# A graph network on one Trainium2 core: which copies and additions of edge counts wait for each other in the first layer's loop

## The chip, the core and the metric

The kernel runs on one core of a Trainium2 chip. The metric is the time of one execution on the device in microseconds; the time given for a kernel is the median of several runs. A profiled execution is a run of its own and takes longer than the others, so durations from it are compared with its own time.

## What is computed

3125 nodes carry rows of 256 numbers, and 100,000 edges (src, dst) join them. The edges arrive sorted by dst, with far more edges at low numbers of dst. Four layers follow each other, each added to its input: a graph attention network of two attention layers, a mixture of experts with one routing for all nodes, two graph convolutions, and a mixture of experts that routes each node. The change lies in the first attention layer and in what it shares with the later ones:

```python
h = (x @ W).reshape(N, H, C)                       # H = 4 heads
e = leaky_relu(al_s[src] + al_d[dst], 0.2)
alpha = exp(e - m[dst]) / segment_sum(exp(e - m[dst]), dst)
out = segment_sum(h[src] * alpha[:, :, None], dst) + bias
```

The later attention layer and the convolutions need only how often each pair (src, dst) occurs. The first layer's loop makes that table of counts while it also forms the first layer's sums.

## The kernel before

`FirstLayer.run` (L2093) holds the loop. Three kinds of work are woven together in it, step by step.

*Counting.* The edges are cut into 391 chunks of 256. Since dst is sorted, the edges of one chunk fall into a narrow window of dst: 8, 14 or 20 columns wide, by the chunk's number (`width`, L80). `make` (L1663) writes two one-hot tiles for a chunk: hot_key (which block of 128 src nodes, and which column of the window) on VectorE (DVE, L1669), and hot_lo (which node within the block) on DVE (L1672) for every third chunk and the first 20, and otherwise on ScalarE (ACT, L1675 and L1678). `multiply` (L1681) multiplies the two on TensorE (PE) into one of three PSUM banks, ps; the product holds the chunk's counts, 128 partitions by 25 blocks by the window's columns. Two instructions bring it into the running table acc, in float16. `keep` (L1697) copies all columns of the window but the first to their place on ACT (L1703); nothing was there before, because the edges are sorted. `add` (L1705) adds the first column on DVE (L1708), because the chunk before may have counted in that column too. The window's place is read from a table into a register when the kernel runs, so the code that sets the waits doesn't know which columns are touched: it sees two instructions that both write somewhere in acc.

`count_step(i)` (L1738) puts them in this order: make chunk i, multiply chunk i-1, add chunk i-3, copy chunk i-2. So each addition waits for the copy just before it, which is that of its own chunk, and each copy waits for the addition just before it, which is that of the chunk before. A bank of ps is free for another product once its addition has read it.

The table is made in ten pieces of 320 dst columns. At the first chunk of a piece `keep` calls `piece` (L1650), which clears a new acc tile on DVE (L1659) and copies over the 100 columns that the old one holds beyond its end (L1661). The finished piece has the nodes' own edges added (`add_own`, L1710) and is stored (`store_counts`, L1719).

*Edges.* For the 283 chunks from number 108 on, `edge_step` (L1883) sums the first layer directly. GpSimd (POOL) fetches the rows of the edges' src (L1797), SyncE (SP) loads windows of terms (L1807, L1810). Four chunks make a batch. For a batch DVE forms the places (L1820, L1823), PE picks the terms (L1831), DVE adds them (L1840, L1843), ACT takes their exponential edge_p (L1844), and DVE spreads it (L1849). For each chunk PE multiplies (L1863, L1869) and DVE adds the sums (L1880). Finished pieces go through the first weights (`through_w1`, L1956), whose results ACT copies out (L1999).

*Dense part.* Once the first piece of counts is stored, 100 steps (`dense_step`, L2077) handle the first 256 dst nodes: exponentials on ACT (L2029, L2031), a product with the counts on DVE (L2036), and a multiplication on PE (L2045).

In the loop each pass calls `count_step`, one waiting task, and as many edge and dense steps as are due, until all are through; counting ends first. The instructions of PE, DVE and ACT are chained in exactly the order in which they are written (`in_order`, L108), so an engine never goes around an instruction that waits. In front of the loop the same `count_step` is called 20-odd times among the layer's preparations; there only DVE's order is fixed by hand. Among those preparations are the exponential of own_w on ACT (L1614), its store to loops, and its loads from there.

Of the kernel before, what the change touches and what calls it, by code (L numbers as in the profile page):

```python
# [17 lines left out]
ALU = mybir.AluOpType  # L18
AX = mybir.AxisListType
PSUM = bass.MemoryType.PSUM  # L20
SYNC = mybir.DependencyInfo(mybir.DependencyClass.Sync, mybir.DependencyReason.DATA)
# [58 lines left out]
def width(c):  # L80
    return next(w for a, e, w in WIN if a <= c < e)
# [7 lines left out]
class Kernel:  # L89
    def __init__(self, ctx, tc):  # L90
        self.tc, self.nc = tc, tc.nc
        nc = self.nc
        self.const = const = ctx.enter_context(tc.tile_pool(name="const", bufs=1))
        self.dram = ctx.enter_context(tc.tile_pool(name="dram", bufs=1, space=DRAM))
        self.ident = const.tile([P, P], F32, name="ident")
        make_identity(nc, self.ident)
        self.eps = const.tile([P, 1], F32, name="eps")
        nc.vector.memset(self.eps, EPS)


        self.rows = const.tile([P, NB, D + 1], F32, name="x_rows")
        self.x = self.rows[:, :, :D]

        self.counts = self.dram.tile([NB, P, NP], F32, name="counts")

        self.counts_t = self.dram.tile([NB, P, NB, P], F32, name="counts_t")
# [1287 lines left out]
class FirstLayer:  # L1394
# [10 lines left out]
    def __init__(self, k, I):  # L1405
        self.k, self.nc, self.tc, self.I = k, k.nc, k.tc, I
        self.table = k.dram.tile([NP, D + 8], F32, name="table")
        self.terms = k.dram.tile([1, NP * 4], F32, name="terms")

        self.places = k.dram.tile([NC, CE], F32, name="places")  # L1410

        self.turned = k.dram.tile([P, 2, NP], F32, name="x_turned")
        self.loops = k.dram.tile([NP - DN, 4], F32, name="loops")
        self.inverse = k.dram.tile([AS, 4, GA], F32, name="inverse")
        self.first = k.dram.tile([4, P, 2, NP], F32, name="first_out")
        self.deg_row = k.dram.tile([NB, P], F32, name="deg_row")
        self.tasks, self.regs, self.counted = deque(), {}, False

# [273 lines left out]
        return g, o  # L1694


    def keep(self, c):  # L1697
        g, o = self.place_of(c)
        if c == CUT[g] and g:
            self.piece(g)  # L1700
            self.tasks.appendleft(lambda: self.store_counts(g - 1))
            self.tasks.appendleft(lambda: self.add_own(g - 1))
        self.nc.scalar.copy(self.acc[g][:, :, ds(o + 1, width(c) - 1)], self.parts[c][:, :, 1:])  # L1703

    def add(self, c):  # L1705
        g, o = self.place_of(c)
        col = self.acc[g][:, :, ds(o, 1)]
        self.nc.vector.tensor_tensor(col, col, self.parts.pop(c)[:, :, 0:1], ALU.add)  # L1708

    def add_own(self, g):  # L1710

# [379 lines left out]


    def run(self, src_cols, dst_cols, dst_rows, x_in, keep, stats, u2):  # L2093

        tc, nc, k, I = self.tc, self.nc, self.k, self.I
# [606 lines left out]
```

## Time and profile before

| what | value |
| --- | --- |
| median of 3 runs | 2530.82 us (2530.34 to 2532.02) |
| the profiled execution's own time | 2636.26 us |
| its span, first to last instruction | 2634.5 us |
| mean granted TensorE clock in it | 0.931 |
| PE busy over the span | 2263.8 us (86%) |
| DVE busy | 1376.1 us (52%) |
| ACT busy | 1153.5 us (44%) |
| POOL busy | 833.4 us (32%) |
| first and last copy of counts (L1703) | 68.9 and 1076.7 us |
| 391 copies L1703 | 178.1 us busy, 455 ns each |
| 391 additions L1708 | 256 ns each (median) |
| 782 one-hots hot_key L1669 | 324 ns each between 60 and 1077 us |
| 494 first halves of hot_lo on ACT, L1675 | 391 ns each |
| 247 second halves, L1678 | 416 ns each |
| 782 products L1686 | 356 ns each |

How to read it: an engine is busy while it executes an instruction; the time before an instruction in which its engine stood idle is given with what ended it, found from the semaphores. A line such as "ACT acc L1703 <- DVE acc L1708: 111.9, 80, 17.6" says that ACT, before its instruction of line 1703 that writes acc, stood idle for 111.9 us in total, in 80 cases, at most 17.6 us, until DVE's instruction of line 1708 ended. In a timeline a line gives start and length in us, engine, line, operation, what it writes and reads, and in brackets the idle time ahead of it. PEld is TensorE's loading of weights; a q behind an engine's name means its sequencer, which handles register operations and separate waits while the engine itself is idle or at work on something earlier.

### The profile page before, as it was taken

Reading aid. Unit: us, or ns where it says so; the run is one execution under the profiler, and the core shown is the slowest. Engines: PE = TensorE matmul, PEld = TensorE weight load, DVE = VectorE, ACT = ScalarE, POOL = GpSimd, SP = SyncE. Lnnn points to the kernel's source line nnn. Section 1 sums busy time; section 2 is a strip of 40 time slices with the busy share of each in tenths; the row PEclk is TensorE's granted clock in tenths of the full one; section 3 lists DMA queues with packets and bytes.
Section 4 is the critical chain, followed back from the end, with each engine's and each line's share of the span. In section 5 each row is a group of like instructions: output and inputs, shape, how many; then the busy total and the mean of one; then the engine's idle time right before and its main releaser. Section 6 shows DMA issues by size and latency. Waiting matters only on the chain. (4 is left out here: it accounts for less than half of the span.)

```text
span 2634.5 us, 38636 instructions
## 1 busy us (share of the span) xinstructions
PE 2263.8 (86%) x11821; PEld 1827.0 (69%) x11821; DVE 1376.1 (52%) x4332; ACT 1153.5 (44%) x2553; POOL 833.4 (32%) x805
## 2 busy tenths in 40 slices
PE   4277789888888888598999989979999998999997
PEld 4155566666666665387888768868877666888886
DVE  6666657466776786514888833433335654111110
ACT  3167655545555554342444434543433434222221
POOL 1465566666676775010000030000001122212221
PEclk9977988888989998899999989989999988999998
DMA  6633446464656665499221110004324426666662
GB/s 219 88 103 89 128 108 183 114 179 119 173 158 175 190 175 149 131 378 304 81 75 63 50 36 0 1 31 145 114 100 139 140 100 195 168 186 180 175 193 54
DMA packets 241723, 354.97 MB, mean 135 GB/s; under 512 B 45360, under 2 KB 182931, under 8 KB 237794
## 3 DMA queue, kind: packets, MB, share of 16 engines
q1 hardware_dynamic: 197762, 253.10, 30.6%
q0 software_dynamic: 40176, 94.81, 14.2%
q10 hardware_dynamic: 3568, 4.47, 0.7%
q8 instruction: 99, 1.62, 0.3%
q14 instruction: 118, 0.97, 0.1%
HBM read 266.60 MB, written 86.86 MB: 134 GB/s over the span
## 5 line engine op out<-in xcount | busy, mean ns | idle before, releaser
L1797 POOL DMA_INDIRECT edge_rows<-table,pick x566 | 608.7, 1075 | 320.2 <-PE edge_sums L1863 107.6
L1863 PE MATMUL edge_sums<-edge_moves,edge_rows 128*128 128x120 f32 x2264 | 351.6, 305 | 37.1 <-DVE agg L1880 30.6
L1863 PEld LDWEIGHTS edge_sums<-edge_moves,edge_rows 128*128 128x128 f32 x2264 | 327.2, 217 | 74.3 <-DVE agg L1880 41.6
L1092 PE MATMUL po<-parts,cnt_r 128*128 128x512 f32 x1250 | 328.2, 416 | 9.4 <-ACT cnt_r L1086 9.4
L1686 PE MATMUL ps<-hot_key,hot_lo 128*128 128x350 f16 (+2 forms) x782 | 205.3, 356 | 106.1 <-DVE acc L1708 49.2
L1703 ACT CAST acc<-ps 128x325 f32 (+2 forms) x391 | 178.1, 455 | 255.5 <-DVE acc L1708 111.9
L1092 PEld LDWEIGHTS po<-parts,cnt_r 128*128 128x128 f32 x1250 | 239.4, 197 | 70.6 <-ACT cnt_r L1086 10.2
L854 PE MATMUL po<-h,w 128*128 128x257 f32 x1250 | 277.5, 382 | 6.7 <-DVE w L845 4.4
L854 PEld LDWEIGHTS po<-h,w 128*128 128x128 f32 x1250 | 236.5, 191 | 43.1 <-DVE w L845 6.4
L1669 DVE TENSOR_SCALAR hot_key<-iota_key,key 128x350 f16<-128x350 f16 (+2 forms) x782 | 231.5, 324 | 34.1 <-PE ps L1686 25.6
L2578 ACT ACTIVATE hid<-ph,ffn_b 128x256 f32<-128x256 f32 x232 | 109.9, 474 | 298.2 <-PE ph L2576 298.2
L2576 PE MATMUL ph<-xe,ffn_w 128*128 128x256 f32 x928 | 210.1, 382 | 2.0 <-DVE xe L2555 2.0
L2586 PE MATMUL py<-ffn_w,hid 128*128 128x256 f32 x928 | 209.5, 384 | 0.0
L2590 POOL DMA_INDIRECT out<-y,to x58 | 90.4, 1558 | 350.1 <-DVE y L2589 269.1
L2576 PEld LDWEIGHTS ph<-xe,ffn_w 128*128 128x128 f32 x928 | 173.9, 191 | 28.9 <-DVE xe L2555 2.2
L2586 PEld LDWEIGHTS py<-ffn_w,hid 128*128 128x128 f32 x928 | 176.5, 193 | 23.4
L1686 PEld LDWEIGHTS <-hot_lo 128*128 128x128 f16 x782 | 62.4, 104 | 160.0 <-issue 60.4
L839 ACT ACTIVATE z<-z,att_cols 128x640 f32<-128x640 f32 x125 | 103.1, 828 | 153.0 <-DVE z L837 130.1
L1675 ACT ACTIVATE hot_lo<-iota_key,lo 128x128 f16<-128x128 f16 x494 | 169.0, 391 | 0.0
L1880 DVE TENSOR_TENSOR agg<-agg,edge_sums 128x126 f32 (+1 forms) x283 | 87.0, 307 | 145.4 <-PE edge_sums L1869 43.9
L1086 ACT CAST cnt_r<-cnt_h 128x1920 fp32r<-128x1920 f16 x50 | 89.9, 1799 | 133.4 <-PE po L1092 130.4
L2045 PE MATMUL po<-x_rows,w 128*128 128x257 f32 x400 | 129.5, 451 | 3.6 <-issue 3.6
(403 smaller groups left out, 3368.2 us busy)
## 6 DMA issues: line engine op xcount, KB each, us to landing
ffn_w<-in_L_ffn_W SPq DMA_DIRECT2D x58, 1024.0 KB
cnt_h<-cnt SPq DMA_DIRECT2D x50, 800.0 KB
rows<-blank SPq DMA_DIRECT2D x109, 258.0 KB
cnt<-acc SPq DMA_DIRECT2D x50, 400.0 KB
cnt<-cnt SPq DMA_DIRECT2D x25, 800.0 KB
normed<-first_out SPq DMA_DIRECT2D x20, 640.0 KB
first_out<-first SPq DMA_DIRECT2D x56, 192.0 KB
edge_rows<-table,pick POOLq DMA_INDIRECT x566
```

The costliest lines, as they stand in the source:

```text
L854: nc.tensor.matmul(pos[i][:, :D + 1], lhsT=w[:, ts(i, P)], rhs=moving[:, j, :D + 1], start=(j == 0), stop=(j == NB - 1))
L1092: nc.tensor.matmul(pos[b], lhsT=c[:, j - j0, ts(b, P)], rhs=parts[i][:, j].rearrange("p a m -> p (a m)"), start=(j == 0), stop=(j == NB - 1))
L1669: nc.vector.tensor_scalar(h[:, u, :NB * w], self.wide[:, :NB * w], self.key[:, t:t + 1], None, op0=ALU.is_equal)
L1675: nc.scalar.activation(l[:, u, :], self.wide[:, :P], AF.Abs, bias=self.lo[:, t:t + 1], scale=-1.0)
L1686: self.nc.tensor.matmul(ps[:, :n], lhsT=l[:, u, :], rhs=h[:, u, :n], start=(u == 0), stop=(u == CT - 1))
L1703: self.nc.scalar.copy(self.acc[g][:, :, ds(o + 1, width(c) - 1)], self.parts[c][:, :, 1:])
L1797: self.nc.gpsimd.indirect_dma_start(out=self.ring[:, e % (RB * BT), :], out_offset=None, in_=self.table, in_offset=bass.IndirectOffsetOnAx ...
L1863: nc.tensor.matmul(ps[:, f * 4 * w:f * 4 * w + EW], lhsT=self.rows_of(m)[:, e, ts(f, P)], rhs=self.spread[m % 2][:, e * 4 * w:e * 4 * w + EW],
L2045: self.nc.tensor.matmul(self.pos[i][:, :D + 1], lhsT=w[:, ts(i, P)], rhs=self.k.rows[:, j, :], start=(j == 0), stop=(j == NB - 1))
L2576: nc.tensor.matmul(ph, lhsT=w1[:, c, ts(f, P)], rhs=xe[:, c, :], start=(c == 0), stop=(c == 1))
L2578: nc.scalar.activation(hid[:, f, :], ph, AF.Gelu, bias=b1[:, f:f + 1])
L2586: nc.tensor.matmul(py, lhsT=hid[:, f, ts(i, P)], rhs=w2[:, f, :], start=(f == 0), stop=(f == NF - 1))
```

## The change

Copies and additions are put into a group named "columns", whose members no longer wait for each other on account of acc. In place of that, each addition is told by name to wait for two copies: that of its own chunk and that of the chunk ahead of it (c-1). Copies are told to wait for no addition. The wait of a copy for its matmul, of both for `piece`, and of anything outside the group for them stays as it was. No instruction that computes is added or left out, and the order in which the functions are called is the same.

```diff
@@ -1414,7 +1414,7 @@
         self.inverse = k.dram.tile([AS, 4, GA], F32, name="inverse")
         self.first = k.dram.tile([4, P, 2, NP], F32, name="first_out")
         self.deg_row = k.dram.tile([NB, P], F32, name="deg_row")
-        self.tasks, self.regs, self.counted = deque(), {}, False
+        self.tasks, self.regs, self.kept, self.counted = deque(), {}, {}, False
 
 
 
@@ -1694,18 +1694,27 @@
         return g, o
 
 
+
+
     def keep(self, c):
         g, o = self.place_of(c)
         if c == CUT[g] and g:
             self.piece(g)
             self.tasks.appendleft(lambda: self.store_counts(g - 1))
             self.tasks.appendleft(lambda: self.add_own(g - 1))
-        self.nc.scalar.copy(self.acc[g][:, :, ds(o + 1, width(c) - 1)], self.parts[c][:, :, 1:])
+        self.kept[c] = self.nc.scalar.copy(self.acc[g][:, :, ds(o + 1, width(c) - 1)],
+                                           self.parts[c][:, :, 1:])
+        self.tc.declare_no_dep(self.kept[c].ins, group="columns",
+                               reason="no copy takes an earlier window's first column")
 
     def add(self, c):
         g, o = self.place_of(c)
         col = self.acc[g][:, :, ds(o, 1)]
-        self.nc.vector.tensor_tensor(col, col, self.parts.pop(c)[:, :, 0:1], ALU.add)
+        ins = self.nc.vector.tensor_tensor(col, col, self.parts.pop(c)[:, :, 0:1], ALU.add)
+        self.tc.add_to_no_dep_group("columns", ins.ins)
+        for b in (c - 1, c):
+            if b >= 0:
+                self.tc.add_manual_dep(ins.ins, self.kept[b].ins.name, SYNC)
 
     def add_own(self, g):
 
```

## The prediction

> **What bounds the kernel now.** I began with the busy time by stretch of the first layer's loop (the columns are the stretch, its length, then busy us and count of PE, PEld, DVE, ACT and POOL, the granted clock, the DMA share and GB/s):
>
> ```profile
> 136.00:215.00 79.00, 60.67 (x394) 48.22 (x394) 54.40 (x265) 54.67 (x177) 46.84 (x47) 0.76 0.37 97
> 215.00:300.00 85.00, 63.06 (x444) 46.22 (x442) 58.98 (x269) 58.34 (x181) 48.17 (x46) 0.84 0.41 113
> 300.00:500.00 200.00, 165.44 (x1105) 129.82 (x1103) 116.12 (x443) 107.31 (x291) 128.58 (x126) 0.88 0.49 134
> 900.00:1077.00 177.00, 146.42 (x945) 108.04 (x944) 130.84 (x399) 95.08 (x241) 103.77 (x103) 0.92 0.55 159
> ```
>
> No engine is full. From 136 to 300 us PE, DVE and ACT are each busy for 69 to 77% of the time and wait for each other in turn; from 300 us PE, at 83%, is nearest to a bound. Then the waits of ACT from 60 to 1077 us (us in total, times, longest):
>
> ```profile
> ACT acc L1703 <- DVE acc L1708: 111.9, 80, 17.6
> ACT edge_p L1844 <- DVE edge_p L1843: 74.8, 42, 6.2
> ACT acc L1703 <- DVE acc L1661: 20.9, 8, 4.7
> ```
>
> The first line is what the change removes; the other two stay. 111.9 us is not a gain: ACT has slack. So I asked who is late because ACT is. From 136 to 300 us PE's waits and DVE's read:
>
> ```profile
> PE ps L1686 <- ACT hot_lo L1678: 10.6, 17, 1.1
> PE ps L1686 <- DVE acc L1708: 8.9, 12, 2.1
> PE ps L1686 <- ACT hot_lo L1675: 2.7, 3, 1.1
> ```
> ```profile
> DVE acc L1708 <- ACT acc L1703: 11.3, 24, 2.6
> ```
>
> Last, I followed the chain of waits back from 1077 us, where counting ends, at each step to what released it. It runs through a copy (L1703) 63 times; 16 of these copies were released by an addition (L1708). Two cases from the timeline. One pays:
>
> ```profile
> 268.56 0.25 DVE L1708 TENSOR_TENSOR acc<-acc,ps 128x25 f32 x1
> 268.90 0.46 ACT L1703 CAST acc<-ps 128x325 f32 x1 [0.71 <-DVE acc L1708]
> 269.24 0.69 ACT L1675 ACTIVATE hot_lo<-iota_key,lo 128x128 f16<-128x128 f16 x2
> 269.96 0.42 ACT L1678 ACTIVATE hot_lo<-hot_lo 128x256 f16<-128x256 f16 x1
> 270.43 0.47 PE L1686 MATMUL ps<-hot_key,hot_lo 128*128 128x350 f16 x2 [1.11 <-ACT hot_lo L1675]
> ```
>
> The copy waits 0.71 us for an addition of the chunk before it, the one-hot behind it is late, and PE stands for 1.11 us. One doesn't:
>
> ```profile
> 970.34 0.24 DVE L1708 TENSOR_TENSOR acc<-acc,ps 128x25 f32 x1
> 970.68 0.55 ACT L1703 CAST acc<-ps 128x475 f32 x1 [3.30 <-DVE acc L1708]
> 970.90 0.19 DVE L1843 SCALAR_TENSOR_TENSOR edge_p<-edge_p,edge_rows 128x32 f32<-128x32 f32 x1
> 971.19 0.23 ACT L1844 ACTIVATE edge_p<-edge_p 128x32 f32<-128x32 f32 x1
> 971.33 0.68 ACT L1675 ACTIVATE hot_lo<-iota_key,lo 128x128 f16<-128x128 f16 x2
> ```
>
> Without its 3.30 us the copy ends earlier, but ACT's next instruction needs DVE's L1843, which ends at 971.09.
>
> [...] everything behind the copy at 970.68 stood with it. [...] DVE's sequencer dealt with the waits of L1840 from 604.94 to 605.29 us, while L1840 itself started at 605.75.
>
> **The change part by part.**
>
> *Copies lose the wait for DVE.* In the built program only copies at the starts of pieces still have one (behind L1661). Each of the 16 links can save at most the lesser of two times: how long ACT stood idle before the copy, and how long the copy's matmul had been done. From 136 to 300 us there are 11 links, 2.43 + 0.69 + 0.04 + 0.48 + 0.68 + 0.68 + 0.39 + 0.77 + 0.39 + 0.71 + 0.79 = 8.05 us. At the first, 139.7 us, PE stood only 0.87 us for ACT afterwards, so 0.87 replaces 2.43: 6.5 us. The upper end is PE's whole wait for ACT's one-hots there, 10.6 + 2.7 = 13.3 us, if ACT gets far enough ahead. I take 8 us, near the lower end: the 6.5 counts one chain alone, and ACT also gets ahead off it (22 such waits, 14.7 us, in this stretch), but a parallel chain may be close behind. From 300 us there are 5 links, 0.07 + 0.89 + 3.30 + 1.46 + 2.96 = 8.7 us. The three large ones are caught again: at 971 and 853 us by the exponential L1844, at 603 us by PE's need for L1823, which DVE, never idle there, ends at 604.60. I take 1 us; the ends are 0 and 8.7.
>
> *Additions.* They waited for their own copy before and still do; the copy of the chunk ahead (c-1) is earlier on ACT and costs nothing. But a wait that used to be implied, for DVE's own previous addition, is now explicit: 297 additions get a separate wait instruction on DVE, and ACT loses 202 of 307. Their prices are in the records by line:
>
> ```profile
> L1840 DVEq EVENT_SEMAPHORE  x279: 21/50/50, 121.1 to 1056.1; - x140
> L1703 ACTq EVENT_SEMAPHORE  x307: 17/17/4519, 69.8 to 1076.7; - x154
> ```
>
> 297 x 0.05 = 14.9 us on DVE's sequencer; ACT's 202 x 0.017 = 3.4 us less. The addition waited for stands at least three DVE instructions back, two hot_key of about 0.3 us between, so it is done and the 0.05 us lies under their work. I take 0; the ends are 0 and 14.9. Queued behind it are DVE's L1880 and the next chunk's one-hots, which PE waits for.
>
> *Order.* PE and POOL keep theirs. On ACT two copies move ahead of the table load and exponential of L1614 (94.04 us). Their matmuls end by 92.9, so own_w comes about 0.5 us later, and the DMA of loops, on the chain to 115 us, with it: 0.5 us lost. On SP two loads swap places with stores; 0, ends -0.5 and 0.5.
>
> *Sum.* 8 + 1 - 0.5 = 8.5 us of the profiled execution's 2636.3 us (span 2634.5). The median without profiling is 2530.8, or 0.96 of it: 8.2 us, 2522.6 us. After 1077 us nothing changes and everything starts earlier.
>
> **The rivals.**
>
> *ACT gets a real lead.* For it: the lockstep was within one step, and three PSUM banks allow more. PE's waits for one-hots go wholly up to 300 us and by half after it (15.0 us there at L1678): 13.3 + 7.5 = 20.8, times 0.96 is 20 us: 2511. Against it: L1844 ties ACT to DVE 71 times.
>
> *The waits are replaced.* ACT's idle time moves to L1844 and to copies waiting for PE, and PE stands for DVE's L1880 instead (30.6 us of PE's waits after 300 us). Gain about 2 us: 2529. For it: the three large links; against it: the 11 small ones.
>
> *The added waits cost: slower.* Where DVE has just stood idle its sequencer has no lead, and each 0.05 us falls on the hot_key and L1880 behind it. At 14.9 us against 8.5 gained the kernel is 6.4 x 0.96 = 6 us slower: 2537. It decides from 8.5/0.05 = 170 uncovered waits of 297 on. Against it: only 68 additions have DVE idle before them, and there the copy is what is late.
>
> That the change doesn't remove the waits is ruled out by the built program.
>
> **How the numbers follow.** Forecast 0.47 (its own range 2514 to 2525.7); lead 0.16; replaced 0.24; slower 0.13. A measurement here tells about 0.2%, 5.1 us. Faster: 0.47 + 0.16 = 0.63; within: 0.24; slower: 0.13. The range 2507 to 2533 leaves out the far part of the lead case and most of the slower one, under 0.2 together.
>
> **What would show it.** Right: ACT's wait of L1703 for L1708 gone, PE's waits for hot_lo from 136 to 300 us down from 13.3 to under 7, and the last count (1077 us) about 8 us earlier, nearly all of it won before 300 us. Wrong: the waits are gone but L1844's grow by as much; L1708 starts later with DVE's sequencer behind it; or most of the gain comes after 300 us. A lower PE clock from 136 to 300 us than 0.76 and 0.84 would take back part of it.

## The result and the profile after

The changed kernel takes 2516.81 us (median of 5 runs, 2510.95 to 2522.96), the kernel before 2530.82 us (5 runs beside them, 2515.80 to 2532.93): a ratio of 0.9947, 95% interval 0.9926 to 0.9968. That is 14.0 us less, where 8.2 were forecast; by the interval it can be 8 to 19 us.

One caution comes first. The kernels ran on several chips, and the unchanged kernel takes 2639 us on one and 2534 or 2535 us on two others, with different granted clocks in the counting loop (each was used once, so chip and occasion can't be told apart). The profile of before that the prediction reads (2636.3 us, clock 0.80 from 136 to 300 us) is of the first kind, the profile of after (2510.95 us, clock 0.98) of the second. These two profiles cannot be set against each other line by line. So the unchanged kernel was profiled again on a chip of the second kind, beside the changed one, and the changed one once more on another such chip; below these are called the second and the third chip.

The changed kernel's busy time by stretch (columns as in the prediction; the last line is the last 177 us of counting, which now ends at 952 us):

```profile
136.00:215.00 79.00, 60.65 (x526) 45.84 (x526) 64.18 (x342) 68.68 (x226) 58.27 (x61) 1.00 0.45 122
215.00:300.00 85.00, 69.20 (x544) 52.51 (x542) 64.38 (x285) 65.67 (x191) 56.95 (x54) 0.96 0.48 134
300.00:500.00 200.00, 174.91 (x1259) 139.19 (x1259) 139.34 (x516) 119.06 (x328) 152.10 (x146) 0.94 0.61 171
775.00:952.00 177.00, 155.95 (x1038) 115.76 (x1037) 139.44 (x424) 102.48 (x262) 118.74 (x118) 0.96 0.63 182
```

From 136 to 215 us PE executes 526 matmuls with the busy time of the prediction's 394: each is shorter, 115 against 154 ns on average, at a clock of 1.00 against 0.76 (both a little too high, for a reason that the next section gives). Then ACT's waits, for the kernel before (second chip, 60 to 1077 us) and for this profile of the changed one (60 to 960 us):

```profile
ACT acc L1703 <- DVE acc L1708: 137.9, 113, 18.4
ACT edge_p L1844 <- DVE edge_p L1843: 90.0, 59, 5.3
...
ACT acc L1703 <- PE ps L1686: 8.4, 13, 1.5
```
```profile
ACT edge_p L1853 <- DVE edge_p L1852: 155.2, 62, 22.0
...
ACT acc L1705 <- PE ps L1686: 40.6, 36, 15.3
ACT acc L1705 <- DVE acc L1661: 13.4, 6, 5.1
```

The copy (now L1705) no longer waits for the addition (now L1713). What grew is the wait of the exponential of `edge_p` (before L1844, now L1853), from 90.0 to 155.2 us, and the copy's wait for its own matmul, from 8.4 to 40.6 us. Where the prediction showed a copy that stood 0.71 us for an addition, one chunk later in the order the same stretch now reads:

```profile
239.43 0.25 DVE L1713 TENSOR_TENSOR acc<-acc,ps 128x25 f32 x1
...
239.57 0.42 ACT L1678 ACTIVATE hot_lo<-hot_lo 128x256 f16<-128x256 f16 x1
...
239.89 0.41 ACT L1705 CAST acc<-ps 128x325 f32 x1
...
240.20 0.69 ACT L1675 ACTIVATE hot_lo<-iota_key,lo 128x128 f16<-128x128 f16 x2
```

There is no bracket behind the copy, as none of its lines shows idle time: ACT goes from one-hot to copy to one-hot without a pause.

PE's and DVE's waits from 136 to 300 us: PE's in the kernel before (second chip) and in the changed kernel (third chip), then DVE's in the first profile of the changed kernel:

```profile
PE ps L1686 <- ACT hot_lo L1678: 19.5, 30, 1.3
PE ps L1686 <- DVE acc L1708: 7.7, 15, 2.3
```
```profile
PE ps L1686 <- ACT hot_lo L1678: 15.5, 26, 0.9
PE ps L1686 <- DVE acc L1713: 8.4, 15, 2.3
```
```profile
DVE acc L1713 <- ACT acc L1705: 15.5, 34, 2.2
```

PE's wait for the one-hots of L1678 fell by a fifth only (on the second chip by a third, to 13.2 us), although the loop became much faster. Summed waits do not show the gain; the stretch also holds more chunks afterwards. It shows when the same chunks are set side by side.

### The profile page after: what moved, and what is told of

It reads as the page before. It is cut to its first block, busy times and chain, and to the rows that moved or that the text cites. A ratio compares the mean times of both kernels' runs of the same rounds, so it can differ in the third digit from the quotient of the medians.

```text
span 2509.2 us, 38737 instructions
## 1 busy us (share of the span) xinstructions
PE 2199.6 (88%) x11821; PEld 1784.2 (71%) x11821; DVE 1369.9 (55%) x4332; ACT 1146.5 (46%) x2553; POOL 834.5 (33%) x805
## 5 line engine op out<-in xcount | busy, mean ns | idle before, releaser
L1806 POOL DMA_INDIRECT edge_rows<-table,pick x566 | 609.8, 1077 | 203.8 <-issue 76.2
L1872 PE MATMUL edge_sums<-edge_moves,edge_rows 128*128 128x120 f32 x2264 | 319.9, 287 | 20.2 <-DVE agg L1889 20.1
L1872 PEld LDWEIGHTS edge_sums<-edge_moves,edge_rows 128*128 128x128 f32 x2264 | 299.4, 200 | 50.1 <-DVE agg L1889 28.4
L1092 PEld LDWEIGHTS po<-parts,cnt_r 128*128 128x128 f32 x1250 | 238.4, 196 | 70.1 <-ACT cnt_r L1086 10.2
L1686 PE MATMUL ps<-hot_key,hot_lo 128*128 128x350 f16 (+2 forms) x782 | 194.4, 334 | 96.0 <-DVE acc L1713 61.1
L1705 ACT CAST acc<-ps 128x325 f32 (+2 forms) x391 | 176.9, 452 | 79.7 <-PE ps L1686 40.6
L845 DVE TENSOR_TENSOR w<-z,cnt 128x640 f32<-128x640 f32 x125 | 106.4, 852 | 37.9 <-PE po L854 35.0
```

Source lines behind the costliest of these rows:

```text
L845: nc.vector.tensor_tensor(w, zs.pop(t), cnts[u, g, j // 5][:, j % 5, :], ALU.mult)
L1092: nc.tensor.matmul(pos[b], lhsT=c[:, j - j0, ts(b, P)], rhs=parts[i][:, j].rearrange("p a m -> p (a m)"), start=(j == 0), stop=(j == NB - 1))
L1686: self.nc.tensor.matmul(ps[:, :n], lhsT=l[:, u, :], rhs=h[:, u, :n], start=(u == 0), stop=(u == CT - 1))
L1705: self.kept[c] = self.nc.scalar.copy(self.acc[g][:, :, ds(o + 1, width(c) - 1)], self.parts[c][:, :, 1:])
L1806: self.nc.gpsimd.indirect_dma_start(out=self.ring[:, e % (RB * BT), :], out_offset=None, in_=self.table, in_offset=bass.IndirectOffsetOnAx ...
L1872: nc.tensor.matmul(ps[:, f * 4 * w:f * 4 * w + EW], lhsT=self.rows_of(m)[:, e, ts(f, P)], rhs=self.spread[m % 2][:, e * 4 * w:e * 4 * w + EW],
```

## The same chunks side by side

The copies number the chunks: the start of the n-th copy says how far the loop is. In us, for the kernel before and after on the second chip (the numbers begin at 0, so 390 is the last):

| copy | before | after | won |
|---|---|---|---|
| 20 | 133.2 | 131.5 | 1.7 |
| 73 | 203.6 | 192.7 | 10.9 |
| 120 | 261.5 | 243.9 | 17.6 |
| 128 | 276.1 | 258.1 | 18.0 |
| 200 | 454.7 | 438.1 | 16.6 |
| 280 | 667.4 | 655.3 | 12.1 |
| 390 | 976.7 | 958.5 | 18.2 |

The gain is made in the first piece of the counts (chunks 0 to 127); behind it the lead varies by 6 us and ends where it was. Now the busy time of the chunks 20 to 73 and 73 to 120, in the kernel before (second chip) and in the changed one (third chip):

```profile
133.20:203.60 70.40, 54.86 (x370) 42.90 (x370) 51.98 (x243) 50.61 (x165) 46.10 (x46) 0.81 0.41 113
203.60:261.50 57.90, 46.02 (x339) 34.93 (x337) 43.82 (x214) 46.41 (x148) 35.08 (x37) 0.85 0.38 97
```
```profile
131.50:193.00 61.50, 46.13 (x372) 36.04 (x372) 50.66 (x246) 50.36 (x167) 47.59 (x46) 0.97 0.48 126
193.00:244.20 51.20, 39.33 (x337) 28.66 (x337) 41.75 (x214) 46.15 (x147) 34.64 (x37) 1.00 0.42 108
```

The instructions are the same in number, and ACT's busy time is the same (50.61 and 50.36; 46.41 and 46.15). PE's time without work is the same too: 70.40 - 54.86 = 15.5 us and 61.50 - 46.13 = 15.4 us, then 11.9 and 11.9 us. The whole difference, 8.9 and 6.7 us, is PE's busy time, 8.7 and 6.7 us less. (With the changed kernel's profile from the second chip, where PE is busy for 46.22 of 61.20 and 40.50 of 51.20 us, PE's busy time makes up 14.2 of 15.9 us.) The matmul of L1863 (L1872 after) takes 337 ns on average in the chunks 20 to 127 before and 293 ns after. PE does the same work at a higher granted clock.

The clock column of these lines is too high, though. A profile has records of the granted clock only from some point on, here from 145.9 us before and from 144.1 us after, and the view counts time without a record as full clock. In that time the matmuls of L1863 (L1872 after) take 421 ns, as in the steps recorded at half clock, where at full clock they take 275 ns. So PE also ran at half clock in some 12.7 us at the start of these chunks, before and after alike; from this I estimate that 0.81 and 0.97 are really 0.72 and 0.87. The difference between the two kernels stays.

How the clock rose can be followed in steps of 3.41 us, the length in which it changes. The kernel before, from 180 us (same columns; the first number after the comma is PE's busy time, the third from the end the clock):

```profile
183.40:186.82 3.42, 1.51 (x14) 0.71 (x12) 2.75 (x15) 2.77 (x10) 2.48 (x3) 1.00 0.43 114
186.82:190.23 3.41, 3.41 (x20) 3.05 (x20) 1.87 (x11) 2.12 (x8) 0.81 (x1) 0.50 0.21 54
190.23:193.64 3.41, 3.41 (x21) 2.81 (x20) 2.77 (x13) 2.51 (x9) 2.02 (x3) 0.50 0.35 104
193.64:197.06 3.42, 3.00 (x27) 2.36 (x26) 2.78 (x15) 2.94 (x11) 2.59 (x3) 1.00 0.40 96
197.06:200.47 3.41, 2.42 (x21) 1.78 (x20) 2.96 (x17) 2.41 (x9) 2.16 (x3) 1.00 0.39 109
200.47:203.88 3.41, 2.50 (x16) 1.64 (x16) 2.06 (x12) 2.62 (x10) 1.89 (x2) 0.50 0.47 121
```

The clock is either full or half. A step in which PE works little (1.51 of 3.42 us) is followed by two steps at half clock; there PE is busy without a gap (3.41 of 3.41) and the others wait for it (DVE's and ACT's busy time drops at first); then the clock is full again, and two steps later PE once more waits for the others. From the first record on, up to copy 127, the kernel before spends 44.4 us at half clock, in six such spells of 3.4, 6.8 or 10.2 us. In all six, the step ahead of the spell had PE busy for 44 to 72%, 59% on average; recorded steps at full clock that were followed by full clock had 55 to 96%, 76% on average. The changed kernel on the third chip, from 185 us:

```profile
185.08:188.49 3.41, 2.29 (x21) 1.62 (x20) 3.13 (x19) 3.31 (x11) 2.50 (x4) 1.00 0.33 99
188.49:191.91 3.42, 2.57 (x22) 1.78 (x20) 1.89 (x10) 2.40 (x9) 2.51 (x4) 1.00 0.49 132
191.91:195.32 3.41, 2.06 (x18) 1.44 (x18) 2.77 (x16) 3.02 (x10) 2.21 (x3) 1.00 0.43 110
195.32:198.73 3.41, 3.01 (x30) 2.54 (x30) 3.09 (x17) 3.28 (x12) 2.06 (x3) 1.00 0.35 89
```

It spends 3.4 us of the recorded time up to copy 127 at half clock, in one spell (6.8 us in two spells on the second chip). With the time before the first record, half clock takes 57.1 us of these chunks in the kernel before, 16.0 and 19.7 us in the changed one. The fourteen profiles of this case together, the kernel before, the changed one and all variants, give for the recorded steps at full clock from copy 20 to 127:

| PE busy in the step | followed by full clock | followed by half clock |
|---|---|---|
| under 50% | 0 | 18 |
| 50 to 60% | 13 | 26 |
| 60 to 75% | 122 | 22 |
| 75% and more | 149 | 0 |

The records show two levels only, 0.50 and 1.00, and every spell in the first profile of each kernel but the last one, with which the record ends, lasts a whole number of 3.41 us (164 of 166 spells). Half clock followed steps in which PE was busy for up to 72% in the kernel before on the second chip. The traces do not give a sharp limit: above, a step of 2.06 of 3.41 us (60%) was followed by full clock. Nor does one busy step always bring full clock back: at 186.82 us PE was busy throughout, and the next step was still at half clock.

## The experiments

Twelve runs followed, four on each of three chips, in this order. The diffs are against the changed kernel, except where the text says otherwise. "Freed" means that a copy no longer waits for additions; an addition told to wait for its two copies by name stays so in all of them. Ratios are to the unchanged kernel on the same chip; they are those of the record, with its 95% intervals, and not exactly the quotients of the two medians.

**Which copies matter, on the first chip** (the unchanged kernel takes 2639.36 us there, median of 75 runs). First the kernel before once more, with no edit, as a measure of the spread:

> The kernel before, unchanged, for a second profile. The first one was taken in an execution of 2636 us with a granted TensorE clock of 0.80 between 136 and 300 us, while the profile of the changed kernel shows 0.98 there. If that low clock belonged to that one execution: time 2515 to 2533 us, clock in that stretch 0.95 or more, last copy of counts at 960 to 972 us, some 8 to 20 us after the changed kernel's 952. If the low clock belongs to this kernel: about 0.80 again, and the last copy near 1077 us. Ratio 1.000 within 0.003, which also shows how far this comparison can be trusted.

Measured 2642.33 us, ratio 1.0008 (0.9995 to 1.0021); the last copy starts at 1079.8 us.

Only the copies of the first piece freed (chunks 0 to 127):

```diff
-        self.tc.declare_no_dep(self.kept[c].ins, group="columns",
-                               reason="no copy takes an earlier window's first column")
+        if c < CUT[1]:
+            self.tc.declare_no_dep(self.kept[c].ins, group="columns",
+                                   reason="no copy takes an earlier window's first column")
```

> Only the 128 copies of the first piece (before about 290 us) are freed from the additions; the other 263 wait as before. My theory, that the gain is won where PE, DVE and ACT are all some 70 to 75% busy and wait for each other in turn: two thirds of the gain or more, ratio 0.9947 to 0.9965. The rival, that the gain goes with the amount of waiting taken away (14.7 us of 72 before 300 us, the rest later): a quarter of it or less, ratio 0.9985 to 1.000.

Measured 2634.94 us, ratio 0.9992 (0.9978 to 1.0006).

Only the copies behind it freed (`if c >= CUT[1]:` in that place):

> The complement: the 263 copies after the first piece are freed, the first 128 wait as before. My theory: the large waits there are caught again by the exponential of edge_p and by DVE's own work, so a third of the gain or less, ratio 0.998 to 1.000. The rival, gain by amount of waiting removed: three quarters or more, ratio 0.9945 to 0.996. If both this and the complement give nearly nothing, the gain needs a lead that is kept through the whole loop.

Measured 2642.21 us, ratio 0.9999 (0.9982 to 1.0015).

Every second copy freed (`if c % 2:`):

> Only copies of chunks with odd numbers are freed; those with even numbers wait for the addition before them as before. If the gain is a sum of single links, each worth its own stall: about half of it, ratio 0.997 to 0.998. If it comes from ACT getting ahead over several chunks: a lead ends at every second chunk, so a quarter or less, ratio 0.9985 to 1.000.

Measured 2638.63 us, ratio 0.9989 (0.9974 to 1.0004).

None gained what the change had gained (0.9947), and this looked at first like a refutation of the whole. The waits of ACT from 136 to 300 us tell part of it. The kernel before, then the first piece freed, both on this chip:

```profile
ACT acc L1703 <- DVE acc L1708: 10.1, 16, 2.4
ACT acc L1703 <- PE ps L1686: 10.0, 11, 2.2
ACT acc L1703 <- PE edge_sums L1863: 8.0, 7, 2.0
```
```profile
ACT acc L1705 <- PE edge_sums L1873: 16.9, 10, 3.4
ACT acc L1705 <- PE ps L1686: 7.3, 11, 2.0
...
ACT acc L1705 <- PE aux L1841: 3.0, 2, 2.6
```

The wait for DVE is gone and waits for PE have grown in its place: over all of PE's lines 19.8 us become 30.6. These sums are rough. On this chip the profiles hold only part of the semaphore events: of the updates by DVE's instructions between copies 20 and 390, 951 of 1654 in the kernel before, against 1619 of 1654 on the second chip. A wait can so be put down to the wrong instruction. The clock doesn't depend on them. From copy 20 to 127 PE is at half clock for 75.1 us in the kernel before and for 76.0 us with the first piece freed (64.9 us recorded, in nine spells, and 11.1 us ahead of the first record, with matmuls of 421 ns). Here freed copies do not keep the clock up, and they gain nothing that can be measured. All copies freed at once were not run on this chip.

**The pair, on the second chip** (unchanged: 2535.25 us, median of 20 runs). The changed kernel and the kernel before once more, both without an edit:

> The changed kernel again, beside the kernel before on one chip. The four runs so far fell on a chip whose granted TensorE clock is 0.76 to 0.80 between 136 and 300 us in every profile, and the kernel before takes 2639 us there; the first measurement of the change fell on one where it takes 2530. On a chip of the slow clock: if the gain is the sum of its two halves (0.9992 and 0.9999, both within noise) 0.9985 to 1.0; if freeing all copies is worth more than its halves, 0.993 to 0.997. On a chip of the fast clock: 0.993 to 0.997 as before.

Measured 2517.50 us, ratio 0.9918 (0.9905 to 0.9931).

> The kernel before, for a profile on the same chip as the run above. Ratio 1.000 within 0.002. On a chip of the fast clock its clock between 136 and 300 us is 0.95 or more and its last copy lies at 960 to 972 us; then its lines can be set against the changed kernel's of 952 us. On one of the slow clock: the last copy near 1078 us.

Measured 2534.56 us, ratio 0.9997 (0.9982 to 1.0012). The first piece freed alone, the same edit as on the first chip:

> Only the first 128 copies freed, as in the run of that name. If TensorE's clock is what hid the gain there (at 0.78 of the clock PE, not the lockstep, sets the pace before 300 us), it appears on a chip of the fast clock: ratio 0.9945 to 0.997; on one of the slow clock again 0.998 to 1.000. If the gain doesn't come from this stretch: 0.999 to 1.001 on either.

Measured 2516.45 us, ratio 0.9923 (0.9908 to 0.9939): all of the gain. The later copies bring nothing, and ACT's waits from 60 to 1077 us show why. First piece freed, then all freed:

```profile
ACT edge_p L1854 <- DVE edge_p L1853: 106.4, 58, 23.3
ACT acc L1705 <- DVE acc L1714: 75.9, 67, 3.7
```
```profile
ACT edge_p L1853 <- DVE edge_p L1852: 160.2, 62, 23.2
...
ACT acc L1705 <- PE ps L1686: 40.2, 35, 15.3
```

Freeing them takes away 75.9 us of waiting for additions, and 160.2 - 106.4 = 53.8 us come back at the exponential, which needs DVE's product of the same edges.

The last of this group keeps the changed waits and gives DVE another order, the addition of chunk i-3 ahead of the one-hots of chunk i, so that an addition which still waits for its copy holds them up:

```diff
+        if 3 <= i <= C1 + 2:
+            self.add(i - 3)
...
-        if 3 <= i <= C1 + 2:
-            self.add(i - 3)
```

> The changed kernel with one more edit: in each counting step DVE's addition of chunk i-3 comes ahead of the one-hots of chunk i, so the bank of ps is free for PE earlier by two to four DVE instructions, 0.6 to 1.1 us. In the changed kernel PE's products still wait for additions 61.1 us in all, so if these waits set the pace: faster than the changed kernel by 3 to 15 us, ratio to before 0.989 to 0.994. If instead DVE then stands for ACT's copy, which has less time to finish: equal or slower than the changed kernel, 0.995 to 1.004.

Measured 2524.64 us, ratio 0.9954 (0.9940 to 0.9968): slower than the changed kernel, faster than the one before. DVE's and PE's waits from 136 to 300 us:

```profile
DVE acc L1713 <- ACT acc L1705: 28.8, 45, 2.0
```
```profile
PE ps L1686 <- DVE hot_lo L1672: 8.6, 14, 2.3
...
PE ps L1686 <- DVE acc L1713: 1.0, 4, 0.3
```

DVE now stands for ACT twice as long (15.2 us in the changed kernel on this chip), and PE waits for DVE's one-hot instead of DVE's addition. Yet up to copy 127 no half clock is recorded (the records begin at 147.1 us), and the chunks 20 to 127 take 121.4 us against 120.1 in the changed kernel and 136.7 before. Of the 4.0 us by which the last copy is later than in the changed kernel, 3.1 are there by copy 20.

**Single links, a lead, or the clock, on the third chip** (unchanged: 2533.68 us, median of 56 runs). The clock had risen in just the stretch where time was won, so it could be cause or company. Freed are the chunks 0 to 72 (`if c < 73:`):

> Only the copies of the chunks 0 to 72 are freed. Two cases, by the granted clock that the kernel before shows on this chip. Where PE's clock from 136 to 300 us is high enough that PE is not the bound (before near 2535 us): if each link of the lockstep is worth its own time, about 10 of the 18 us won by chunk 120 are kept (chunks 20 to 73 took 9.2 us less with all free), ratio 0.996. If a higher granted clock from 136 to 215 us is the cause, everything is won by chunk 73 and the chunks behind it are as fast as in the kernel before, which is the same 0.996, but then chunks 73 to 120 must take 57.9 us in this run and show waits of copies for additions as before; a lead, once won, would carry them through in under 55 us. Where the clock is low (before near 2639 us): 0.999 to 1.001.

Measured 2525.16 us, ratio 0.9968 (0.9957 to 0.9978). Then the chunks 73 to 127 (`if 73 <= c < CUT[1]:`):

> Only the copies of the chunks 73 to 127 are freed, where the granted clock was alike before and after (0.92 and 0.94). If the copies' wait is the cause: chunks 73 to 120 take 51 to 52 us in place of 57.9, and 6 to 7 us stay at the end, ratio 0.997. If the clock from 136 to 215 us was the cause, nothing is won: 0.9995 to 1.0005. Where the clock is low (before near 2639 us): 0.999 to 1.001.

Measured 2526.14 us, ratio 0.9967 (0.9955 to 0.9978). Every second copy (`if c % 2:`):

> Every second copy is freed. If the gain is a sum of single links, half of the waits go and half of the 18 us: 0.996. If what counts is a lead of several chunks, each copy that is still tied ends it and little is won: 0.998 to 1.000. Where the clock is low (before near 2639 us): 0.9989 as in the first run of this kernel.

Measured 2525.04 us, ratio 0.9968 (0.9955 to 0.9980). And the changed kernel without an edit:

> The changed kernel again, as the measure for the three others on this chip. Where the kernel before takes near 2535 us: 0.992. Where it takes near 2639 us, with PE's clock under 0.8 from 136 to 300 us: 0.998 to 1.000, since the kernel with the first piece alone freed gave 0.9992 there and the later pieces 0.9999; if the whole gain came there too, the pieces would have to act only together.

Measured 2516.98 us, ratio 0.9933 (0.9917 to 0.9949).

The two parts make up the whole: 0.9968 x 0.9967 = 0.9935 against 0.9933. Every second copy gives half. That speaks against a lead of several chunks that a single tied copy would end; the freed copies add up. What two of my expectations rested on fell, however: that the clock from 73 to 120 is alike before and after. It is alike only in stretches cut by time; cut by chunks it was 0.85 and 1.00. The clock goes with the copies that are freed, in either half. The chunks 20 to 73 and 73 to 120 with 0 to 72 freed, then with 73 to 127 freed:

```profile
131.20:192.20 61.00, 45.00 (x374) 34.47 (x375) 49.86 (x248) 50.37 (x167) 46.77 (x46) 1.00 0.48 130
192.20:250.70 58.50, 45.16 (x335) 33.40 (x334) 43.64 (x213) 46.34 (x147) 34.82 (x37) 0.85 0.37 96
```
```profile
133.00:200.70 67.70, 52.20 (x369) 40.22 (x369) 51.28 (x241) 50.40 (x165) 46.50 (x46) 0.80 0.43 113
200.70:252.50 51.80, 42.17 (x339) 31.59 (x339) 41.80 (x213) 46.40 (x148) 34.67 (x36) 0.93 0.40 107
```

Where copies are freed the clock is 1.00 (an estimated 0.91 with the time before the first record at 142.4 us) and 0.93, and the chunks take 61.0 and 51.8 us, as with all freed (61.5 and 51.2). Where they are tied it is 0.80 (so estimated, 0.78) and 0.85, and they take 67.7 and 58.5 us, near the kernel before (70.4 and 57.9). The clock is the company of the freed copies: where they end, half clock is back (17.1 us of the chunks 73 to 120, as in the 17.3 us of the kernel before).

## Why the prediction was right, and where its size came from

*Which copies, and where.* Right. It put nearly all of the gain before 300 us; on the second chip 18.0 of 18.2 us are won by copy 128, and freeing the first piece alone gives the whole.

*"I take 8 us, near the lower end."* This term was mis-sized: the chunks 20 to 127 take 136.7 us before and 120.1 us after on the second chip, 16.6 us, twice the term and above its upper end of 13.3. The sum priced waits and held each instruction's duration fixed. The chain of waits in the new profile of before gives no more than the old one (14 such links up to 289 us, with 8.3 us of idle time ahead of their copies), so the profile of the slower kind is not what misled here, although it holds only 947 of DVE's 1654 semaphore updates between copies 20 and 390. What was missing, by the traces, is that with the freed copies PE's granted clock rises (half clock for 57.1 us of the chunks 20 to 127 before, 16.0 and 19.7 us after), and with it change the matmuls that the sum took as given (L1863: 337 ns on average before, 293 ns after). The prediction named the clock only as a danger and didn't see that the change itself could move it. How much of the 16.6 us is due to it is open. In the kernel before a chunk takes 1.41 us at half clock and 1.20 us at full clock; at full clock in the changed kernel it takes 1.09 us (all on the second chip, with the time before the first record counted as half clock). An estimate from these: at the changed kernel's pace the 66 chunks done at full clock before would have saved some 7 us with no change of clock, which is near the term of 8, and the rest goes with fewer chunks at half clock. The prediction's sign that PE's wait for the one-hots would fall under 7 us failed: of 19.5 us at L1678, 13.2 to 16.5 are left in the three profiles of the changed kernel.

*"I take 1 us" from 300 us on.* From copy 128 to 390 it is 700.6 us before and 700.3 us after on the second chip (696.0 in the first profile of the changed kernel): near 0, within the ends given. The reason named, that the exponential L1844 catches the copies, is what the waits show.

*Additions at 0.* Right, and the price of a wait was too high. The records of the two lines in the changed kernel (on the sequencers; ns least, median and most):

```profile
L1713 DVEq EVENT_SEMAPHORE  x297: 21/21/21, 70.0 to 954.7; - x149
...
L1705 ACTq EVENT_SEMAPHORE  x105: 17/17/4515, 69.3 to 951.8; - x105
```

297 waits of 21 ns, 6.2 us in all, not 14.9; and DVE's idle time ahead of L1713 is there put down to ACT's copies (32.3 us) and one-hots (0.8 us), none of it to issue. The slower rival needed 170 uncovered waits; in this profile there is one, the last: the other 296 run on the sequencer while DVE is still at work on something earlier. No run leaves out an addition's wait for its own chunk's copy; that it is needed is not shown.

*Order, -0.5 us.* It did not show. The exponential of `own_w` starts at 94.45 us before and after: two more copies stand ahead of it, but the copies already run earlier (number 10 at 91.0 in place of 92.8 us). SP's swap of loads and stores was not tried by itself.

*The sum.* The factor 0.96 is wrong. Being profiled doesn't lengthen an execution here: the profiled ones took 2637.45 us beside a median of 2642.33 on the first chip, and 2534.24 beside 2534.56 on the second. The 2636.3 us belong to the slower kind of chip. Without the factor the forecast would have been a gain of 8.5 us in place of 8.2, which changes little.

*The rivals.* "A real lead" (2511 us) lay as near to the measured 2516.8 us as the forecast did; as a mechanism every second copy giving half speaks against it. "The waits are replaced" is what happens behind the first piece, and, as far as its profiles tell, on the first chip too.

*Luck.* The lines were read in a profile of the slower kind of chip, where the two halves of the change gave nothing measurable (0.9992 and 0.9999), and the result was taken on the other kind. Had it been taken there, these halves suggest little or no gain. And the repeats, 17.8 and 16.7 us less on the second and third chip, are about twice the forecast; the total held because the stated range reached down to 2507 us.

What stays open. That freeing the copies of the first piece causes the gain on the second and third chip is shown, piece by piece. That much of it comes by way of the clock is the reading of the traces and not shown: PE's unoccupied time stays nearly as it is and its busy time falls; and on the chip where the clock stays low (75.1 and 76.0 us at half clock in the chunks 20 to 127) the halves of the change gain nothing. A direct test would fill PE's pauses in the kernel before with matmuls whose results nobody reads, and see whether the clock stays up; it was not tried. Against the clock as the whole account speaks that chunks at full clock became faster too (1.20 to 1.09 us): shorter waits alone may do that, or the end of the to and fro of PE late and PE waiting. Nor is the clock all that sets the first chip apart: in the kernel before a chunk takes 1.41 us there at full clock, against 1.20. And another sign in the kernel before: where DVE already stood idle when the last of a chunk's matmuls L1869 ended by the profile, its addition L1880 of these sums began within 0.06 us in all 49 cases on the second chip; on the first it began more than 0.1 us later, and up to 0.65 us, in 6 of 31. What makes that chip late, and why it keeps the low clock with the copies freed, is not known.

## What to carry to other kernels

Where PE's granted clock in a stage is under 1, a wait of a side engine may cost more than itself (on the second chip the waits were priced at 8 us, and 16.6 us were won): look at steps of a few us (3.41 us here) for the pattern of PE waiting, then half clock, then PE saturated, and price the matmuls at both durations (275 and 421 ns here). Check by those durations that the clock is recorded at all in the stretch. Compare chunk by chunk, not by stretches of time, which mix different work, and compare profiles of one kind of chip. And expect little from freeing an engine where a second tie of the same engine stands close behind: 75.9 us of waits removed after the first piece brought no gain that can be seen.

## What the runs showed of the hardware that was not expected

The same kernel takes 2639 us on one chip and 2534 to 2535 us on two others, about 4% apart, with medians of 75, 56 and 20 runs; the difference arises in counting (the last copy at 1080 and 977 us), most of it behind the first piece (794.9 and 700.6 us from copy 128 to 390). On both kinds, a matmul of L1863 has the same two durations (medians), 275 ns at full and 421 ns at half clock; what differs in the clock is how often the half clock is granted (75.1 and 57.1 us of the chunks 20 to 127). And the half clock comes without any long pause of PE: between copies 20 and 127 of the kernel before on the second chip PE never stands for more than 2.3 us at a time, while the clock changes in steps of 3.4 us. What goes with it is PE's busy share of the step ahead: under 50% was followed by half clock in 18 of 18 steps, 75% and more in none of 149.
